# Transposes as 32x32 blocks through DRAM, half-width slice tokens and a table of steps for the order, in an f32 attention layer on one core

## The chip, the cores and the metric

One core of one Trainium2 chip. The time is the device time of one execution in microseconds (us), as a median over the runs of a kernel. Every kernel here gives the reference's result within the tolerance. Ratios are the mean time of one kernel's fast runs over that of the other's fast runs of the same rounds, so they are not quite the ratio of the medians quoted beside them.

## The reference, cut to what matters

For each of 32 batches x is 512 tokens by 256 features, f32. Two stages, each on a layernorm:

```
out = relu(x @ mlp1_w + b)                       # 512 x 512
out = elu(gat(out, no mask)) + out               # attention 512 x 512 over 512 features
out = relu(out @ mlp2_w + b)                     # 512 x 256
out = relu(elu(gat(out, adj)) + out)             # masked attention over 256 features
x   = x + out

w      = softmax((x @ W_x) @ W_slice / temp)     # per head, 8 heads x 64 slices
tokens = (w^T @ (x @ W_fx)) / (sum of w + 1e-5)  # 64 x 64 per head
attention among the 64 tokens of a head, then  out = w @ result @ W_out,  x = x + out
```

Every product in this kernel sums over the index that lies on partitions in both operands, so features and tokens have to change places several times in a batch. Those transposes are what the change is about.

## The kernel before: the parts that matter

The program is first recorded as a list of operations. A planner then orders the list: it simulates the five engines with a price for each operation, and on each engine takes the operation with the lowest "turn" among those that could start. The order it finds is fixed in the program; in the traces below each engine works down its own list and waits where something isn't there yet. (In all code cuts, `...` marks what is left out, and most comments are added for the reader.)

```python
class Recorder:
    AHEAD = 3                     # a batch may start while the oldest is at most 3 behind
    ORDERS = (1.0, 1.1, 1.2, 1.3, 1.4), (1.2, 1.4, 1.6), (0.0, 0.1, 0.2)

    def _cost(self, op, out, ins):               # (time on its engine, then time to be done)
        if op.method == "dma_start":
            return 0.1, 2.5 + out.size() * 4 / 180e3
        ...
    def order(self):              # 45 tries of two numbers a batch; the shortest by a replay wins
        ...
```

Most transposes are made on TensorE, written to PSUM and copied out by ScalarE. Two tensors, the first layernorm and the first attention's output, went another way already: VectorE turns 32x32 blocks, four writes put them into DRAM and one read brings them back in place.

```python
    def flip(src, stage, t):                      # 32x32 blocks on VectorE
        nc.vector.transpose(stage[:, :, ts(t, Q)], src.rearrange("p (c i) -> p c i", i=Q))

    def gather(stage, dst):                       # 4 writes to DRAM, 1 read back
        scr = dram.tile([blocks, Q, P // Q, P], F32, ...)
        for a in range(P // Q):
            nc.sync.dma_start(scr[:, :, a, :].rearrange("c r j -> r c j"), stage[ts(a, Q), :, :])
        nc.sync.dma_start(dst, scr.rearrange("(k c) r a j -> (c r) k (a j)", c=P // Q))
    ...
        # masked attention: e is turned by TensorE
            nc.scalar.activation(e, e, AF.Exp, bias=nmax[:, i : i + 1], accum_out=den[:, i : i + 1])
            pt = tr_tile([P, NT, P])
            for j in range(NT):
                nc.tensor.transpose(pt[:, j, :], e[:, ts(j)], ident)
            nc.scalar.copy(pT[:, :, ts(i)], pt)
    ...
        # slice tokens: full width, of which only the diagonal 64x64 blocks are used
        for p in range(NP):
            for k in range(KD):
                nc.tensor.matmul(pm[:, p, :], wfx[:, k, ts(p)], s1T[:, k, ts(p)], ...)
        nc.tensor.matmul(pm, bfx, nrow, start=False, stop=True)
```

## Time and profile before

| | before |
|---|---|
| time, median | 2928.01 us |
| TensorE busy | 98% |
| period of a batch | 88.5 us |
| matmuls a batch | 407 |
| DMA share of the span | 0.19 |
| first output leaves | 228.7 us |
| last masked-attention matmul to the end | 59.5 us |

In the views PE is TensorE, PEld its weight loads, DVE VectorE, ACT ScalarE, POOL GpSimd, and SP SyncE, which issues most transfers. The period is the distance of the output transfers in mid-span; all of it is TensorE work. The prediction shows the lines that say so.

### The profile page before, as it was taken

The numbers are of one execution on the slowest core, as the hardware profiler recorded it, in microseconds if no ns is written. First come the engines' busy times: TensorE is split into PE (matmuls) and PEld (weight loads), VectorE is DVE, ScalarE is ACT, GpSimd is POOL, SyncE is SP. The second block draws the span as 40 slices with busy tenths as digits, with TensorE's granted clock in tenths as the row PEclk, the third lists the DMA queues.
The fourth block names the chain that finished last, engine by engine and source line by source line (L and its number), as shares of the span: only waits on it lengthen the run. The fifth ranks groups of instructions, "written<-read, shape, count | busy, mean of one in ns | idle before, by whom it ended". The sixth has DMA issues, their size and how long they took to land.

```text
span 2926.5 us, 35159 instructions
## 1 busy us (share of the span) xinstructions
PE 2853.9 (98%) x13037; PEld 2187.4 (75%) x13037; DVE 1978.3 (68%) x4694; ACT 1119.3 (38%) x2182; POOL 112.8 (4%) x233
## 2 busy tenths in 40 slices
PE   3999999999999999999999999999999999999997
PEld 3777777777778777778777778777777777777775
DVE  4567776667776666776676866677766677766675
ACT  1433444333443343443333443333433334433432
POOL 1000000000000000000000000000000000000000
PEclk9999999999999999999999999999999999999998
DMA  5112220112211122211122211122201122201110
GB/s 177 44 29 65 65 65 22 52 57 65 65 53 34 44 65 65 65 44 44 44 65 65 65 36 51 44 65 65 65 26 54 51 65 65 61 19 45 43 44 15
DMA packets 185412, 159.34 MB, mean 54 GB/s; under 512 B 9109, under 2 KB 159257, under 8 KB 185241
## 3 DMA queue, kind: packets, MB, share of 16 engines
q1 hardware_dynamic: 181904, 154.96, 18.0%
q10 hardware_dynamic: 3336, 2.14, 0.3%
q8 instruction: 103, 1.69, 0.2%
q14 instruction: 69, 0.56, 0.1%
HBM read 89.96 MB, written 67.11 MB: 54 GB/s over the span
## 4 chain that ended last, share of the span: by engine, by line
PE 95%; DVE 3%; DMA 1%; ACT 0%; issue 0%; SPq 0%; POOL 0%; ACTq 0%; POOLq 0%; DVEq 0%
PE mm L255 85%; PE tr L255 9%; PE sm L255 1%; DVE w L255 1%; DVE mx L255 0%; DVE rs L255 0%; DMA wfx<-in_L_ffn_W_fx_dram 0%; DMA temp<-n_L_ffn_temperature_dram 0%; DVE m L255 0%; DVE u L255 0%; DMA scr<-xn_stage 0%; ACT m L255 0%; DMA xt<-in_x_dram 0%; DVE pT L255 0%; DVE ln_st L255 0%
## 5 line engine op out<-in xcount | busy, mean ns | idle before, releaser
L255 PE MATMUL mm<-wfc,o0T 128*128 128x257 f32 x2048 | 579.0, 381 | 0.0
L255 PE MATMUL mm<-h,pT 128*128 128x257 f32 (+1 forms) x2048 | 454.6, 378 | 0.1
L255 PEld LDWEIGHTS mm<-h,pT 128*128 128x128 f32 x2048 | 386.1, 189 | 80.5 <-issue 13.4
L255 PEld LDWEIGHTS mm<-wfc,o0T 128*128 128x128 f32 x2048 | 363.7, 190 | 53.2 <-issue 16.3
L255 PE MATMUL mm<-gg,wT 128*128 128x256 f32 x1024 | 299.5, 379 | 0.0
L255 PE MATMUL mm<-h,p2T 128*128 128x256 f32 x1024 | 290.8, 379 | 0.0
L255 PE MATMUL mm<-xnT,w 128*128 128x512 f32 x512 | 249.3, 592 | 0.0
L255 PE MATMUL mm<-xn,w 128*128 128x257 f32 x1024 | 246.4, 382 | 0.0
L255 PE MATMUL mm<-o1T,w 128*128 128x512 f32 x512 | 241.2, 592 | 0.0
L255 PE MATMUL mm<-weff,xn2T 128*128 128x512 f32 x512 | 226.7, 596 | 0.7 <-ACT xn2T L255 0.7
L255 DVE COPY h<-mm 128x257 f32<-128x257 f32 (+1 forms) x192 | 81.7, 425 | 208.2 <-PE mm L255 204.2
L255 PEld LDWEIGHTS mm<-gg,wT 128*128 128x128 f32 x1024 | 189.2, 190 | 24.0 <-ACT gg L255 0.2
L255 PEld LDWEIGHTS mm<-h,p2T 128*128 128x128 f32 x1024 | 186.6, 190 | 24.5
L255 PEld LDWEIGHTS mm<-xn,w 128*128 128x128 f32 x1024 | 186.0, 192 | 23.7 <-issue 3.3
L255 PEld LDWEIGHTS mm<-weff,xn2T 128*128 128x128 f32 x512 | 97.8, 191 | 122.9 <-issue 99.8
L255 ACT ACTIVATE m<-m 128x512 f32<-128x512 f32 x192 | 120.9, 630 | 170.7 <-DVE m L255 170.6
L255 DVE SCALAR_TENSOR_TENSOR u<-m,u 128x512 f32<-128x512 f32 x192 | 131.5, 685 | 70.3 <-ACT m L255 70.3
L255 ACT ACTIVATE u<-mm,rd 128x256 f32<-128x256 f32 x192 | 90.3, 470 | 208.0 <-PE mm L255 181.2
L255 ACT COPY h<-mm 128x257 f32<-128x257 f32 (+1 forms) x192 | 71.8, 374 | 227.2 <-PE mm L255 224.7
L255 PE MATMUL mm<-wh,o2T 128*128 128x258 f32 x512 | 155.6, 390 | 0.0
L255 ACT ACTIVATE w<-w 128x512 f32<-128x512 f32 x128 | 80.8, 631 | 187.6 <-DVE w L255 187.6
L255 ACT ACTIVATE o2T<-mm,b 128x512 f32<-128x512 f32 x64 | 44.0, 687 | 263.2 <-PE mm L255 262.9
(141 smaller groups left out, 4396.6 us busy)
## 6 DMA issues: line engine op xcount, KB each, us to landing
scr<-u_stage SPq DMA_DIRECT2D x128, 256.0 KB, 4.0
o1T<-scr SPq DMA_DIRECT2D x32, 1024.0 KB, 5.7
xt<-in_x_dram SPq DMA_DIRECT2D x32, 512.0 KB, 4.6
x<-in_x_dram SPq DMA_DIRECT2D x32, 512.0 KB, 4.1
scr<-xn_stage SPq DMA_DIRECT2D x128, 128.0 KB, 2.4
xnT<-scr SPq DMA_DIRECT2D x32, 512.0 KB, 6.4
out_dram<-x SPq DMA_DIRECT2D x32, 512.0 KB, 3.2
w<-in_L_gnn_mlp_w_dram SPq DMA_DIRECT2D x2, 512.0 KB, 6.8
```

Of the source, the lines that this page charges most:

```text
L255: getattr(getattr(self.nc, op.engine), op.method)(*op.args, **op.kwargs)
```

## The change

The intent is to take work from TensorE, the bound. The transposes of e, xn2, w and s1 leave TensorE for VectorE blocks and DRAM, in the manner of `flip` and `gather`. The masked product is turned round, so that its result comes out with features on partitions. The slice tokens are computed in halves of 64 columns, without the blocks that nobody uses. Copies and scalings move from VectorE to ScalarE, to make room. Left out of the cut below: w takes the buffer of p2T, the staging tiles of u, e and w share one buffer, and the rows of xn2 go through DRAM too, to match the block order. And the search over 45 orders gives way to a table with a turn for each of 23 steps. The core of the diff, with cuts:

```diff
+TURNS = {
+    "load": -152.1, "norm1": 325.7, "mlp1": 467.1, "h": 505.9, "factors": 512.7, "p": 531.2,
+    "pv": 533.5, "o1": 575.4, "mlp2": 575.4, "h2": 619.7, "e": 627.1, "p2": 627.1,
+    "pv2": 700.4, "x1": 718.3, "norm2": 735.4, "w": 763.7, "sums": 777.8, "s1T": 784.5,
+    "tokens": 830.6, "att": 855.6, "vo": 865.1, "gg": 867.3, "out": 893.5,
+}
+PERIOD, SPARE = 118.7, 0.01
...
         if op.method == "dma_start":
-            return 0.1, 2.5 + out.size() * 4 / 180e3
+            return 0.45, 2.2 + out.size() * 4 / 200e3
...
-            pt = tr_tile([P, NT, P])
-            for j in range(NT):
-                nc.tensor.transpose(pt[:, j, :], e[:, ts(j)], ident)
-            nc.scalar.copy(pT[:, :, ts(i)], pt)
+            nc.vector.tensor_scalar(e, e, rd, None, op0=OP.mult)
+            flip(e, stage, i)
+        nc.step = "p2"
+        gather("e", stage, pT)
...
+        for k in range(KD):
+            pm = mm_tile([P, N])
+            for j in range(NT):
+                nc.tensor.matmul(
+                    pm.rearrange("p (t a i) -> p t a i", t=NT, i=Q), h[:, j, ts(k)],
+                    in_order(pT[:, j, :]), start=(j == 0), stop=(j == NT - 1),
+                )
...
-            pt = tr_tile([P, NP, P])
-            for p in range(NP):
-                nc.tensor.transpose(pt[:, p, :], w[:, t, ts(p)], ident)
-            nc.scalar.copy(wT[:, :, ts(t)], pt)
+            flip(wt, stage, t)
+        gather("w", stage, wT)
...
-        for k in range(KD):
-            pt = tr_tile([P, INNER])
-            for p in range(NP):
-                nc.tensor.transpose(pt[:, ts(p)], s1[:, p, ts(k)], ident)
-            nc.scalar.copy(s1T[:, k, :], pt)
+        gather("s1", stage, s1T)
...
+                for s in range(2):
+                    nc.tensor.matmul(
+                        pm[ts(s, C), p, :].rearrange("c (a i) -> c a i", i=Q),
+                        wfx[:, k, ts(2 * p + s, C)], in_order(s1T[:, k, :])[:, p, ts(s, 2), :],
+                        start=(p == 0 and k == 0), stop=False,
+                    )
```

More of the change, by code (lines that the diff above doesn't have):

```diff
@@ L1 @@
 from contextlib import ExitStack
-from itertools import product
 import concourse.bass as bass
@@ L28 @@
     AHEAD = 3
-    ORDERS = (1.0, 1.1, 1.2, 1.3, 1.4), (1.2, 1.4, 1.6), (0.0, 0.1, 0.2)
     def __init__(self, nc):
-        self.nc, self.ops, self.logs, self.age, self.stage = nc, [], {}, -1, 0
+        self.nc, self.ops, self.logs, self.age, self.step = nc, [], {}, -1, ""
         for engine in ENGINES:
@@ L63, in take @@
                 (outs if key in ("out", "accum_out") else ins).append(x)
-        op = _Op(engine, method, args, kwargs, self.age, self.stage, len(self.ops))
+        op = _Op(engine, method, args, kwargs, self.age, self.step, len(self.ops))
         op.cost, op.lag = self._cost(op, outs[0], ins)
@@ L72, in take @@
                 log = self.logs.setdefault(ap.tensor.name, _Log(ap, self.age))
-                op.logs.add(log)
+                if log not in op.logs:
+                    op.logs.append(log)
                 kept = []
@@ L97, in _cost @@
         if op.method == "dma_start":
-            return 0.1, 2.5 + out.size() * 4 / 180e3
+            return 0.45, 2.2 + out.size() * 4 / 200e3
         if op.engine == "tensor":
             one = max(n / 1200 + 0.002, 0.109)
+            if out.ap[0][1] == P // 2:
+                one = max(n / 2400, 0.03)
             return (one if op.method == "transpose" else 2 * one), self.DRAIN
@@ L195, in _schedule @@
         return done
-    def _length(self, ops):
-        free, ready, users, until, slots, held = {}, {}, {}, {}, {}, set()
-        for op in ops:
-            for log in op.logs:
-                users[log] = users.get(log, 0) + 1
-        for op in ops:
-            at = ready.get(op, 0.0)
-            for log in op.logs:
-                if log not in held:
-                    held.add(log)
-                    places = slots.setdefault(log.tag, [0.0] * log.bufs)
-                    places.sort()
-                    at = max(at, places.pop(0))
-            t = free.get(op.engine, 0.0)
-            t = max(t + (0.03 if op.engine == "tensor" and at > t - 0.1 else 0.0), at)
-            free[op.engine], end = t + op.cost, t + op.cost + op.lag
-            for log in op.logs:
-                users[log] -= 1
-                until[log] = max(until.get(log, 0.0), end)
-                if not users[log]:
-                    slots[log.tag].append(until[log] + self.SIGNAL)
-            for later in op.after:
-                if later.engine != op.engine:
-                    at = end + self.SIGNAL
-                else:
-                    at = t + op.cost if op.engine == "tensor" else end
-                ready[later] = max(ready.get(later, 0.0), at)
-        return max(free.values())
     def order(self):
@@ L232, in order @@
         for op in self.ops:
-            stage = op.age, op.stage
-            parts[op] = work.get(stage, 0.0)
-            work[stage] = parts[op] + (op.cost if op.engine == "tensor" else 0.0)
-        best = None
-        for late, long, spare in product(*self.ORDERS):
-            turns = {
-                op: op.age + (late + long * part / work[op.age, 1] if op.stage else
-                              part / (work[op.age, 0] or 1.0))
-                for op, part in parts.items()
-            }
-            try:
-                ops = self._schedule(self.ops, turns.get, spare)
-            except RuntimeError:
-                continue
-            length = self._length(ops)
-            if best is None or length < best[0]:
-                best = length, ops
-        self.length = best[0]
-        return best[1]
+            step = op.age, op.step
+            parts[op] = work.get(step, 0.0)
+            work[step] = parts[op] + (op.cost if op.engine == "tensor" else 0.02)
+        ends = dict(zip(TURNS, list(TURNS.values())[1:] + [max(TURNS.values())]))
+        turns = {}
+        for op, part in parts.items():
+            at = TURNS.get(op.step, 0.0)
+            part /= work[op.age, op.step]
+            turns[op] = op.age * PERIOD + at + part * (ends.get(op.step, 0.0) - at)
+        return self._schedule(self.ops, turns.get, SPARE)
     def emit(self):
@@ L264, in __init__ @@
         self.psum = ap.space == bass.MemoryType.PSUM
-        self.queue = self.tag, age if self.psum else 0
+        self.queue = self.tag, age if self.psum or self.tag.startswith("stage") else 0
         self.entries = []
 class _Op:
-    def __init__(self, engine, method, args, kwargs, age, stage, index):
+    def __init__(self, engine, method, args, kwargs, age, step, index):
         self.engine, self.method, self.args, self.kwargs = engine, method, args, kwargs
-        self.age, self.stage, self.index = age, stage, index
-        self.logs, self.after = set(), []
+        self.age, self.step, self.index = age, step, index
+        self.logs, self.after = [], []
     def __lt__(self, other):
@@ L359, in flip, with gather @@
         )
-    def gather(stage, dst):
+    def gather(what, stage, dst):
         blocks = stage.shape[1]
-        scr = dram.tile([blocks, Q, P // Q, P], F32, name="scr", tag=f"scr{blocks}", bufs=2)
+        scr = dram.tile([blocks, Q, P // Q, P], F32, name="scr", tag=f"scr_{what}", bufs=2)
         for a in range(P // Q):
@@ L474, in adj_ffn_kernel @@
                 )
-    adjt = new("adjt", [P, NT, N], tag="w", dtype=I32)
+    adjt = new("adjt", [P, NT, N], tag="wT", dtype=I32)
     nc.sync.dma_start(adjt, adj.rearrange("(t p) j -> p t j", p=P))
@@ L583, in elu_elu @@
     def elu_elu(parts, m, u):
-        (v0, rd0, cols0), (v1, rd1, cols1) = parts
-        nc.vector.tensor_scalar(u[:, cols0], v0, rd0, None, op0=OP.mult)
-        nc.scalar.activation(u[:, cols1], v1, AF.Copy, scale=rd1)
+        for v, rd, cols in parts:
+            nc.scalar.activation(u[:, cols], v, AF.Copy, scale=rd)
         nc.vector.tensor_scalar(m, u, 0.0, None, op0=OP.min)
@@ L595, in front @@
     def front(b):
-        load_x(b + 1)
+        nc.step = "load"
+        if b:
+            load_x(b)
+        nc.step = "norm1"
         xn = new("xn", [P, NT, D])
@@ L603, in front @@
         xnT = new("xnT", [P, KD, N])
-        gather(stage, xnT)
+        gather("xn", stage, xnT)
+        nc.step = "mlp1"
         o0T = new("o0T", [P, KH, N], bufs=2)
@@ L613, in front @@
             nc.scalar.activation(o0T[:, m, :], pm, AF.Relu, bias=b1[:, m : m + 1])
+        nc.step = "h"
         h = new("h", [P, NT, 2, HH + 1])
@@ L623, in front @@
                     )
-                if s:
-                    nc.vector.tensor_copy(h[:, t, s, :], pm)
-                else:
-                    nc.scalar.copy(h[:, t, s, :], pm)
+                nc.scalar.copy(h[:, t, s, :], pm)
         f1, f2 = h[:, :, 0, HH], h[:, :, 1, HH]
+        nc.step = "factors"
         fm = small("fm", [P, 1])
@@ L657, in front @@
             nc.scalar.copy(acb[:, s, :], pt)
+        nc.step = "p"
         pT = new("pT", [P, NT, N])
         for j in range(NT):
-            nc.vector.tensor_scalar(
-                pT[:, j, :], acb[:, 1, :], ex[:, 3, j : j + 1], None, op0=OP.mult
+            nc.scalar.activation(
+                pT[:, j, :], acb[:, 1, :], AF.Copy, scale=ex[:, 3, j : j + 1]
             )
@@ L667, in front @@
             )
+        nc.step = "pv"
         o1T = new("o1T", [P, KH, N])
-        stage = new("u_stage", [P, HID // Q, P], tag="p2T")
+        stage = new("u_stage", [P, HID // Q, P], tag="stage")
         for i in range(NT):
@@ L683, in front @@
             flip(u, stage, i)
-        gather(stage, o1T)
+        nc.step = "o1"
+        gather("u", stage, o1T)
         for m in range(KH):
@@ L690, in middle @@
     def middle(b, o1T):
+        nc.step = "mlp2"
         o2T = new("o2T", [P, KD, N])
@@ L700, in middle @@
             nc.scalar.activation(o2T[:, m, :], pm, AF.Relu, bias=b2[:, m : m + 1])
+        nc.step = "h2"
         h = new("h2", [P, NT, D + 2])
@@ L707, in middle @@
                 )
-            if t % 2:
-                nc.vector.tensor_copy(h[:, t, :], pm)
-            else:
-                nc.scalar.copy(h[:, t, :], pm)
+            nc.scalar.copy(h[:, t, :], pm)
         f2b = new("f2b", [P, N])
@@ L716, in middle @@
         nc.scalar.copy(f2b, pt)
-        r2 = new("r2", [P, NT, D])
-        for t2 in range(NT // 2):
-            pt = tr_tile([P, 2, D])
-            for s in range(2):
-                for k in range(KD):
-                    nc.tensor.transpose(pt[:, s, ts(k)], o2T[:, k, ts(2 * t2 + s)], ident)
-            nc.scalar.copy(r2[:, ts(t2, 2), :], pt)
         pT = new("p2T", [P, NT, N])
+        nc.step = "e"
+        stage = new("e_stage", [P, N // Q, P], tag="stage")
         den = small("den", [P, NT])
@@ L739, in middle @@
             )
-            pt = tr_tile([P, NT, P])
-            for j in range(NT):
-                nc.tensor.transpose(pt[:, j, :], e[:, ts(j)], ident)
-            nc.scalar.copy(pT[:, :, ts(i)], pt)
-        rd = small("rd2", [P, NT])
-        nc.vector.reciprocal(rd, den)
+            rd = den[:, i : i + 1]
+            nc.vector.reciprocal(rd, rd)
+            nc.vector.tensor_scalar(e, e, rd, None, op0=OP.mult)
+            flip(e, stage, i)
+        nc.step = "p2"
+        gather("e", stage, pT)
@@ L747, in middle @@
         x1 = new("x1", [P, NT, D], bufs=2)
         nc.sync.dma_start(x1, x[b].rearrange("(t p) d -> p t d", p=P))
-        for i2 in range(NT // 2):
-            pm = mm_tile([P, 2, D])
-            for s in range(2):
-                i = 2 * i2 + s
-                for j in range(NT):
-                    nc.tensor.matmul(
-                        pm[:, s, :], pT[:, j, ts(i)], h[:, j, :D],
-                        start=(j == 0), stop=(j == NT - 1),
-                    )
-            u, m = row("u2", (P, 2, D)), row("m2", (P, 2, D))
-            elu_elu(
-                [(pm[:, s, :], rd[:, 2 * i2 + s : 2 * i2 + s + 1], s) for s in range(2)], m, u
-            )
-            nc.vector.tensor_tensor(u, u, r2[:, ts(i2, 2), :], op=OP.add)
+        nc.step = "pv2"
@@ new lines, in middle @@
+        for k in range(KD):
[5 more added lines that the diff above has]
+                )
+            m = row("m2")
+            nc.vector.tensor_scalar(m, pm, 0.0, None, op0=OP.min)
+            nc.scalar.activation(m, m, AF.Exp)
+            nc.scalar.activation(m, m, AF.Exp, bias=neg1)
+            nc.vector.scalar_tensor_tensor(m, m, -1.0, pm, op0=OP.add, op1=OP.max)
+            nc.vector.tensor_tensor(o2T[:, k, :], m, o2T[:, k, :], op=OP.add)
@@ L763, in middle @@
+        nc.step = "x1"
+        for t2 in range(NT // 2):
+            pt = tr_tile([P, 2, D])
+            for s in range(2):
+                for k in range(KD):
+                    nc.tensor.transpose(pt[:, s, ts(k)], o2T[:, k, ts(2 * t2 + s)], ident)
             nc.vector.scalar_tensor_tensor(
-                x1[:, ts(i2, 2), :], u, 0.0, x1[:, ts(i2, 2), :], op0=OP.max, op1=OP.add
+                x1[:, ts(t2, 2), :], pt, 0.0, x1[:, ts(t2, 2), :], op0=OP.max, op1=OP.add
             )
@@ L768, in back @@
     def back(b, x1):
-        xn = new("xn2", [P, NT, D + 1])
+        nc.step = "norm2"
+        xn = new("xn2", [P, NT, D])
+        layernorm(x1, xn, "ln2")
+        stage = new("xn2_stage", [P, D // Q, P], tag="stage4")
+        for t in range(NT):
+            flip(xn[:, t, :], stage, t)
+        xnT = new("xn2T", [P, KD, N])
+        gather("xn2", stage, xnT)
+        scr = dram.tile([NT, P, D], F32, name="scr", tag="rows", bufs=4)
+        nc.sync.dma_start(scr.rearrange("t p d -> p t d"), xn)
+        xn = new("xn2_rows", [P, NT, D + 1])
         nc.gpsimd.memset(xn[:, :, D : D + 1], 1.0)
-        layernorm(x1, xn, "ln2")
-        xnT = new("xn2T", [P, KD, N])
-        transpose_features(xn, xnT)
-        w = new("w", [P, NT, INNER])
+        for t in range(NT):
+            nc.sync.dma_start(xn[ts(t, Q), :, :D], scr[t].rearrange("(a i) d -> i a d", i=Q))
+        nc.step = "w"
+        w = new("w", [P, NT, INNER], tag="p2T")
         wT = new("wT", [P, NP, N])
+        stage = new("w_stage", [P, INNER // Q, P], tag="stage")
         for t in range(NT):
@@ L798, in back @@
             )
-            pt = tr_tile([P, NP, P])
-            for p in range(NP):
-                nc.tensor.transpose(pt[:, p, :], w[:, t, ts(p)], ident)
-            nc.scalar.copy(wT[:, :, ts(t)], pt)
+            flip(wt, stage, t)
+        gather("w", stage, wT)
+        nc.step = "sums"
         s1 = new("s1", [P, NP, D + 1])
+        stage = new("s1_stage", [P, D // Q, P], tag="stage4")
         for p in range(NP):
@@ L814, in back @@
             nc.vector.reciprocal(rn, rn)
-            nc.vector.tensor_scalar(s1[:, p, :], pm, rn, None, op0=OP.mult)
+            nc.scalar.activation(s1[:, p, :], pm, AF.Copy, scale=rn)
+            flip(s1[:, p, :D], stage, p)
+        nc.step = "s1T"
         s1T = med("s1T", (P, KD, INNER))
-        for k in range(KD):
-            pt = tr_tile([P, INNER])
-            for p in range(NP):
-                nc.tensor.transpose(pt[:, ts(p)], s1[:, p, ts(k)], ident)
-            nc.scalar.copy(s1T[:, k, :], pt)
+        gather("s1", stage, s1T)
         pn = sm_tile([NP, P])
         nc.tensor.transpose(pn, s1[:, :, D], ident)
-        nrow = new("nrow", [NP, NP, P])
-        nc.vector.tensor_tensor(
-            nrow, ident[:NP, :NP, None].to_broadcast([NP, NP, P]),
-            pn[:, None, :].to_broadcast([NP, NP, P]), op=OP.mult,
-        )
-        pm = mm_tile([P, NP, P])
+        nrow = new("nrow", [NP, 2, NP, G])
+        for s in range(2):
+            nc.vector.tensor_tensor(
+                nrow[:, s], ident[:NP, :NP, None].to_broadcast([NP, NP, G]),
+                pn[:, None, ts(s, G)].to_broadcast([NP, NP, G]), op=OP.mult,
+            )
+        nc.step = "tokens"
+        pm = mm_tile([P, NP, G])
         for p in range(NP):
             for k in range(KD):
-                nc.tensor.matmul(
-                    pm[:, p, :], wfx[:, k, ts(p)], s1T[:, k, ts(p)],
-                    start=(p == 0 and k == 0), stop=False,
-                )
-        nc.tensor.matmul(pm, bfx, nrow, start=False, stop=True)
+                for s in range(2):
+                    nc.tensor.matmul(
+                        pm[ts(s, C), p, :].rearrange("c (a i) -> c a i", i=Q),
+                        wfx[:, k, ts(2 * p + s, C)], in_order(s1T[:, k, :])[:, p, ts(s, 2), :],
+                        start=(p == 0 and k == 0), stop=False,
+                    )
+        for s in range(2):
+            nc.tensor.matmul(
+                pm[ts(s, C)], bfx[:, ts(s, C)], nrow[:, s], start=False, stop=True
+            )
         def diagonal(dst, src):
@@ L845, in back @@
         tok = new("tok", [P, NP, G])
-        diagonal(lambda s: tok[ts(s, C), :, :], lambda s: pm[ts(s, C), :, ts(s, G)])
+        nc.vector.tensor_copy(tok, pm)
         for s in range(2):
@@ L854, in back @@
             nc.tensor.matmul(psc[:, p, :], qbd[:, p, :], tok[:, p, :], start=True, stop=True)
+        nc.step = "att"
         amax = small("amax", [P, NP])
@@ L867, in back @@
         nc.vector.reciprocal(ra, ra)
+        nc.step = "vo"
         vo = med("vo")
@@ L881, in back @@
         nc.vector.tensor_copy(attT, pt)
+        nc.step = "gg"
         gg = med("gg")
@@ L892, in back @@
                 )
+        nc.step = "out"
         for t2 in range(NT // 2):
@@ L907, in adj_ffn_kernel @@
     for b in range(B):
-        nc.age, nc.stage = b, 0
-        o1T = front(b)
-        nc.stage = 1
-        back(b, middle(b, o1T))
+        nc.age = b
+        back(b, middle(b, front(b)))
     with tc.manual_schedule():
```

## The prediction

> **What bounds the kernel now.** I read the page's busy shares first, then the busy time of two stretches that are one batch long, then the order of the matmuls inside one batch, the groups that the change removes, the groups that it adds more of, and the transfers.
>
> ```profile
> span 2926.5 us, 35159 instructions
> PE 2853.9 (98%) x13037; PEld 2187.4 (75%) x13037; DVE 1978.3 (68%) x4694; ACT 1119.3 (38%) x2182; POOL 112.8 (4%) x233
> ```
>
> ```profile
> 1500.00:1588.50 88.50, 88.50 (x408) 67.95 (x407) 61.38 (x146) 34.90 (x68) 3.42 (x7) 1.00 0.19 54
> 2500.00:2588.50 88.50, 88.50 (x407) 67.94 (x406) 61.28 (x146) 34.90 (x68) 3.41 (x7) 1.00 0.19 54
> ...
> 2870.00:2890.00 20.00, 13.28 (x39) 7.29 (x40) 13.24 (x29) 3.01 (x6) 1.26 (x2) 0.74 0.00 0
> 2890.00:2910.00 20.00, 17.09 (x79) 12.79 (x78) 10.01 (x27) 4.71 (x9) 0.79 (x2) 0.86 0.00 1
> 2910.00:2927.00 17.00, 10.45 (x46) 7.99 (x44) 3.46 (x7) 2.48 (x6) 0.00 (x0) 0.90 0.09 31
> ```
>
> The columns are the stretch, its length, then busy time and count of PE, PEld, DVE, ACT and POOL, the granted clock, and the DMA share and rate. The 13037 matmuls over 32 batches are 407 each, and every 88.5 us stretch holds 407: the period of a batch is 88.5 us, PE is busy all of it, DVE 61.3, ACT 34.9. Thirty-two periods are 2832 us; the other 94 us are 43 us before the first matmul, which waits for weights, and the last batch's thinner end, where PE idles and its clock drops to 0.74. So TensorE's own issue sets the period.
>
> A matmul's duration isn't what it costs the stream; the step between starts is:
>
> ```profile
> 1572.22 7.03 PE L255 MATMUL mm<-weff,xn2T 128*128 128x512 f32 x16
> 1579.09 1.88 PE L255 MATMUL mm<-xnT,w 128*128 128x512 f32 x4
> 1580.81 0.60 PE L255 MATMUL mm<-wfc,o0T 128*128 128x257 f32 x2
> 1581.24 0.60 PE L255 MATMUL tr<-ident,w 128*128 128x128 f32 x4
> 1581.67 1.90 PE L255 MATMUL mm<-xn,w 128*128 128x257 f32 x8
> ```
>
> From start to start: 16 of 512 columns take 6.87 us, 0.429 each; 2 of 257 take 0.43, 0.216 each; 4 transposes take 0.43, 0.108 each. With these steps the 407 matmuls of a batch add up to 87.8 us of the 88.5.
>
> **What the Trainium skill says.** (1) "Perfetto Trace Analysis", section "Identifying the Most-Contended Engine": matmul busy share overstates how near the roofline a kernel is, since matmuls are pipelined; load-weights busy share is the better sign. Here that is 75%, yet the starts are back to back, so I count steps between starts instead. (2) "VectorE: DVE Perf Modes", section "The three transpose paths": VectorE transposes only inside 32x32 blocks. That is why the blocks must be put in place by a transfer through DRAM; the kernel before does so for two tensors already. (3) The same page, "Why PSUM operands drop a tier": a PSUM source loses the double rate of a scalar operation. The trace agrees: the minimum over 512 columns from SBUF takes 415 ns, while a scaling of only 256 columns from PSUM takes 474. (4) "TensorEngine Tiling (Array Packing)", section "Key Properties": changing the tiling mode drains TensorE. A related sign in the trace is the bias product with only four rows: its two matmuls of 512 columns hold the stream 1.05 us (1515.08 to 1516.13) instead of 0.86, with 0.1 us of gap before.
>
> **The change part by part.**
>
> TensorE, removed:
>
> ```profile
> L255 PE MATMUL tr<-ident,w 128*128 128x128 f32 x512 | 78.5, 277 | 9.6 <-DVE rs L255 6.6 <-DVE w L255 2.9
> L255 PE MATMUL tr<-ident,e 128*128 128x128 f32 x512 | 76.8, 273 | 0.0
> ...
> L255 PE MATMUL tr<-ident,s 128*128 128x128 f32 x256 | 43.6, 273 | 0.4 <-DVE s L255 0.3
> L255 PE MATMUL tr<-ident,xn 128*128 128x128 f32 x256 | 39.7, 278 | 9.4 <-DVE xn L255 9.4
> ```
>
> These are 16+16+8+8 = 48 transposes a batch, at 0.108 us 5.2 us. The transposes of o2T stay, moved behind the second attention. The turned masked product is 16 matmuls of 512 columns (6.86 us) in place of 32 of 256 (6.9): nothing. The slice tokens by halves replace 16 matmuls of 128 columns (1.8 us) and the bias pair (1.15 with its gap) by 32 half-width matmuls of 64 columns and 4 half-width bias ones. No trace shows the half-width step. As an estimate between 64/1200 us (half the step of 128 columns) and half of that, if neighbouring halves overlap, the 32 take 0.9 to 1.7 us and the bias 0.4 to 0.9, to which drains are added at each switch of mode: before, this block was interleaved with other work in about six pieces, and at 0.1 to 0.3 us a piece that is 0.6 to 1.8. Net between -1.4 and +1.5; I take -0.5. TensorE goes from 88.5 to about 82.8 us a batch.
>
> VectorE, added:
>
> ```profile
> L255 DVE STREAM_TRANSPOSE u_stage<-u 128x512 f32<-128x512 f32 x128 | 88.9, 695 | 0.3
> ...
> L255 DVE STREAM_TRANSPOSE xn_stage<-xn 128x256 f32<-128x256 f32 x128 | 49.0, 421 | 3.3 <-DMA scr<-xn_stage 3.3
> ```
>
> Four flips each of e and w (8 x 0.695 = 5.56) and of xn2 and s1 (8 x 0.421 = 3.37); the scaling of e (4 x 0.478, from the row that makes pT, = 1.9); three more reciprocals (0.45); the minimum from PSUM (2 x 0.27 = 0.5); nrow in two (0.2). Sum 12.0. Taken away: six scalings of u (6 x 0.474 = 2.8), the copies of h and h2 (4 x 0.425 + 2 x 0.426 = 2.55), the first product of pT (1.9) and the scaling of s1 (1.9). Sum 9.2. VectorE goes from 61.3 to about 64 us, 77% of the new period. ScalarE loses the copies of the transposes of e, w, xn2, s1 and r2 out of PSUM (14 x 0.585 = 8.2), two scalings (0.94) and one copy of tok (0.37), 9.5 in all. It gains 8.9 from what VectorE gave up. It stays near 34 us.
>
> Transfers:
>
> ```profile
> scr<-u_stage SPq DMA_DIRECT2D x128, 256.0 KB, 4.0
> o1T<-scr SPq DMA_DIRECT2D x32, 1024.0 KB, 5.7
> ...
> scr<-xn_stage SPq DMA_DIRECT2D x128, 128.0 KB, 2.4
> xnT<-scr SPq DMA_DIRECT2D x32, 512.0 KB, 6.4
> ```
>
> Out and back, e and w add 2 MB each, xn2 and s1 1 MB each, the rows of xn2 1 MB: 7 MB a batch, 235 MB on 159 MB. The DMA share rises from 0.19 to about 0.47: not a bound. Issues rise from 13 to 38 a batch, at 0.377 us 14 us of SP's time.
>
> What lies on the path is latency. A removed transpose with its copy took about 2.3 us at the end of the trace (s1, from 2897.5 to 2899.9); flip, landing in DRAM and landing in SBUF are 0.4 + 2.4 + 6.4 = 9.2 us for 512 KB and 0.7 + 4.0 + 5.7 = 10.4 for 1 MB. In the steady state four batches are in flight and this is hidden if the order leaves TensorE other work. In the last batch there is none: xn2 and s1 each add about 7 us, the moved transposes 1 to 2; w's transfer lies beside the sums and tokens. The end grows by 16 us. Filling the deeper pipeline I put at 8 us, and leftover bubbles in the steady state, with VectorE busier and an order fixed from modelled times, at 0.4 us a batch, 13 us.
>
> Sum: 2928 - 32 x 5.2 (166) - 32 x 0.5 (16) + 16 + 8 + 13 = 2783; I say 2780 us, 5% less.
>
> **The rivals.** First, a buffer cycle becomes the bound. p2T and w now share one single buffer, and w needs the result of p2T through the norm, so gather of e, second attention, norm, transfer of xn2, slice weights and sums run one after another once a batch. In the steady state before, from the first matmul on p2T (1536.66) to the last of the sums (1591.2) are 54.5 us; add 5.7 for the gather of e and about 8 for xn2's transfer: 69 us of 82.8. It fits with 14 us to spare; for it speaks also that the weights stage keeps its pace though VectorE is shared. Against it: u, e and w flips take turns in one stage buffer, some 18 us each by the trace, and a wait there stretches the cycle. If it becomes 88, the time is 2880 to 2950.
>
> Second, SP issues in order, so one transfer that waits for its data holds all behind it. The page now has the gathers waiting on their own scratch writes; with six gathers a batch, late transfers could cost a few us each: 2 us a batch makes 2850. For it speaks that the order is taken from modelled landings; against it, that modelled landings of 1 MB are longer than the measured 5.7.
>
> Third, the drains of half-width matmuls give back what the transposes saved: at the dear end +1.5 us a batch, 2845.
>
> Fourth, everything fits and the halves overlap: -1.4 in place of -0.5 and no bubbles, 2735.
>
> **Range and chances.** The range 2715 to 2860 holds the fourth rival and the mild forms of the second and third, not a closed buffer cycle. Within 2% begins at 2870. Faster 0.88, same 0.09, slower 0.03.
>
> **What would show it.** Right: about 361 matmuls a batch (407 - 48 - 16 + 18), a period near 83 us with PE busy in nearly all of it, DVE near 64 us, DMA share near 0.47, the chain of waits still almost all PE. Wrong: PE share well under 97% in mid-span with its waits ending at transfers or at w and p2T (first or second rival); gaps or long steps around the products of s1T and wfx (third); a first out transfer much later, or an end longer than some 80 us after the last p2T matmul, would show that fill or tail was misjudged.

## More of the kernel before

Columns: stretch, length, busy time (and count) of PE, PEld, DVE, ACT and POOL, granted clock, DMA share, GB/s.

```profile
1563.00:1587.00 24.00, 24.00 (x94) 15.77 (x93) 22.59 (x55) 11.36 (x19) 2.52 (x4) 1.00 0.43 122
```

## The result, and the profile after

3021.48 us (3016.19 to 3025.93, 4 runs) against 2928.01: a ratio of 1.0319, 95% interval 1.0297 to 1.0340. Slower, where 5% faster was predicted. Page of the changed kernel:

```profile
span 3014.1 us, 33327 instructions
## 1 busy us (share of the span) xinstructions
PE 2784.2 (92%) x11565; PEld 1922.1 (64%) x11565; DVE 2017.3 (67%) x4822; ACT 1095.0 (36%) x2214; POOL 112.8 (4%) x233
```

TensorE has 1472 matmuls fewer, 361 a batch, and still the span is longer: it is busy 92% and no longer 98%. VectorE is busy 39 us longer than before, ScalarE 24 us less. The output transfers are 90.4 us apart in mid-span, where 82.8 was predicted. So what grew isn't work: TensorE stands 230 us of its span in place of 73. The view of waits, longest TensorE ones first (in us: total, times, longest):

```profile
PE mm L225 <- DMA s1T<-scr: 92.5, 32, 12.6
PE tr L225 <- DMA wx<-in_L_ffn_W_x_dram: 37.0, 1, 37.0
PE mm L225 <- DMA p2T<-scr: 25.4, 20, 6.4
PE mm L225 <- DVE pT L225: 24.3, 30, 5.0
```

The second is the start and was there before. The first comes in every batch: TensorE stands 2.9 us for s1T, the turned sums on their way back from DRAM. TensorE's timeline around one such wait (start, length, instruction, idle before it and its releaser):

```profile
1575.65 5.39 PE L225 MATMUL mm<-p2T,h 128*128 128x512 f32 x12 [0.54 <-DMA p2T<-scr]
1583.45 0.45 PE L225 MATMUL mm<-s1T,wfx 128*64 128x64 f32 x8 [2.41 <-DMA s1T<-scr]
1583.83 1.12 PE L225 MATMUL mm<-p2T,h 128*128 128x512 f32 x2
1584.89 0.45 PE L225 MATMUL mm<-s1T,wfx 128*64 128x64 f32 x8
```

TensorE had more to do: two of the p2T matmuls come right after. They stand behind the first s1T products because the planner put them there, and the list is fixed. The two then take 1.06 us from start to start where 0.86 is usual.

Why s1T is late shows in SyncE's timeline of the same stretch (start, time of the issues, transfers):

```profile
1563.46 3.12 SPq L225 DMA_DIRECT2D scr<-w_stage  x4
1566.69 1.12 SPq L225 DMA_DIRECT2D p2T<-scr  x1
1567.94 1.70 SPq L225 DMA_DIRECT2D scr<-s_stage  x2
1570.58 0.79 SPq L225 DMA_DIRECT2D wT<-scr  x1
1571.41 1.28 SPq L225 DMA_DIRECT2D scr<-s_stage  x2
1572.74 3.62 SPq L225 DMA_DIRECT2D scr<-xn_stage  x4
1579.71 0.38 SPq L225 DMA_DIRECT2D s1T<-scr  x1
```

Within ten microseconds come 1 MB of w, two gathers of 1 MB, and the four writes of s1 between them. The s1 writes, 128 KB each, land 7 to 8 us after their issue, and only then can s1T be read back. The list of transfers (KB each, median us to landing) has the same for the whole run:

```profile
p2T<-scr SPq DMA_DIRECT2D x32, 1024.0 KB, 9.0
...
wT<-scr SPq DMA_DIRECT2D x32, 1024.0 KB, 8.9
...
scr<-s_stage SPq DMA_DIRECT2D x128, 128.0 KB, 7.8
```

The prediction had 5.7 us for 1 MB and 2.4 us for 128 KB, from a kernel in which transfers met few others. The stretches of the changed kernel, the burst and the rest of the batch:

```profile
1563.00:1587.00 24.00, 20.74 (x90) 13.90 (x89) 16.21 (x48) 9.47 (x18) 1.37 (x3) 1.00 0.88 257
1587.00:1653.00 66.00, 65.66 (x278) 45.96 (x277) 47.44 (x106) 24.61 (x51) 2.06 (x4) 1.00 0.33 94
```

A mean DMA share of 0.47 is 0.88 for a quarter of the batch and 0.33 for the rest. In the quarter, TensorE is idle 3.3 us; in the rest, 0.3.

**Theory A.** The work did fall as predicted. The order is what fails: the planner prices each transfer as if it were alone (0.45 + 2.2 + 0.66 = 3.3 us for a 128 KB write), puts what reads it that close behind, and the burst makes each landing late by the same amount in every batch.

**Rivals.** B: a cycle through the shared single buffers, or VectorE, holds the period whatever the order is. C: the half-width products drain TensorE at each change of width and give back what the transposes saved. D: the step table is a worse order than the old search.

### The profile page after: what moved, and what is told of

The parts are those of the page before. It is cut to its first block, busy times and chain, and to the rows that moved or that the text cites. A ratio compares the mean times of both kernels' runs of the same rounds, so it can differ in the third digit from the quotient of the medians.

```text
span 3014.1 us, 33327 instructions
## 1 busy us (share of the span) xinstructions
PE 2784.2 (92%) x11565; PEld 1922.1 (64%) x11565; DVE 2017.3 (67%) x4822; ACT 1095.0 (36%) x2214; POOL 112.8 (4%) x233
## 5 line engine op out<-in xcount | busy, mean ns | idle before, releaser
L225 PE MATMUL mm<-h,pT 128*128 128x256 f32 (+1 forms) x2048 | 510.4, 385 | 30.3 <-DVE pT L225 24.3
L225 PE MATMUL mm<-wfc,o0T 128*128 128x257 f32 x2048 | 498.2, 380 | 0.0
L225 PE MATMUL mm<-p2T,h 128*128 128x512 f32 x512 | 265.5, 654 | 35.7 <-DMA p2T<-scr 25.4
L225 DVE SCALAR_TENSOR_TENSOR e<-f2b,h,mbias 128x512 f32<-128x512 f32 x128 | 92.9, 747 | 280.2 <-ACT f2b L225 280.2
L225 PE MATMUL mm<-xn_rows,w 128*128 128x257 f32 x1024 | 259.2, 388 | 13.4 <-DVE w L225 5.5
L225 ACT COPY h<-mm 128x257 f32<-128x257 f32 (+1 forms) x384 | 143.7, 375 | 244.5 <-PE mm L225 236.8
L225 PEld LDWEIGHTS mm<-xn_rows,w 128*128 128x128 f32 x1024 | 198.2, 194 | 47.1 <-ACT w L225 9.1
L225 PEld LDWEIGHTS mm<-p2T,h 128*128 128x128 f32 x512 | 94.6, 200 | 130.6 <-issue 81.0
L225 PEld LDWEIGHTS mm<-o1T,w 128*128 128x128 f32 x512 | 95.8, 191 | 115.5 <-issue 85.0
L225 PE MATMUL mm<-s1T,wfx 128*64 128x64 f32 x1024 | 68.7, 252 | 92.5 <-DMA s1T<-scr 92.5
```

The source lines that it names most:

```text
L225: getattr(getattr(self.nc, op.engine), op.method)(*op.args, **op.kwargs)
```

## The experiments

They were run with the kernel before beside them (medians 2927.76 to 2928.83 us). The changed kernel itself was not run again; times are compared with its 3021.48. Each expectation names its own theories A and B, which are not always the A and B above; where the letters differ, the text says so.

### 1. Slice tokens in full width again

```diff
-                for s in range(2):
-                    nc.tensor.matmul(
-                        pm[ts(s, C), p, :].rearrange("c (a i) -> c a i", i=Q),
-                        wfx[:, k, ts(2 * p + s, C)], in_order(s1T[:, k, :])[:, p, ts(s, 2), :], ...
+                nc.tensor.matmul(
+                    pm[:, p, :].rearrange("c (a i) -> c a i", i=Q),
+                    wfx[:, k, ts(p)], in_order(s1T[:, k, :])[:, p, :, :], ...
```

> The changed kernel with one part undone: the slice tokens again as 8 full-width products (16 matmuls of 128 columns) and one bias product, of which only the diagonal blocks are kept. Theory A (drains at the switches between half-width and full-width matmuls cost about 2.5 us a batch, more than the halves save): about 40 to 70 us faster than the changed kernel, 2950 to 2980 us, while the wait for s1T stays at about 3 us a batch. Theory B (only waits for transfers matter; halves cost what their issue costs): 1 to 1.5 us a batch more TensorE work in the stream, so the same time or 20 to 40 us slower, 3020 to 3060 us.

(Theory A of this expectation is C above, its B is A above.) 3001.55 us (ratio to before 1.0260, 1.0242 to 1.0277), 20 us faster; the period fell from 90.4 to 89.5, the wait for s1T stayed (97.4 us). C has the right sign and a fifth of the size that it would need: in this order the halves cost 0.9 us a batch net. I had expected 40 to 70 us from the drains; the time falls between the two ranges. They can't be the main cause of the loss.

### 2. The writes of s1 from another issuing engine

```diff
-            nc.sync.dma_start(
+            (nc.scalar if what == "s1" else nc.sync).dma_start(
                 scr[:, :, a, :].rearrange("c r j -> r c j"), stage[ts(a, Q), :, :]
```

> The changed kernel, with only the four scratch writes of s1 issued from ScalarE instead of SyncE; same bytes, same order of all else. Theory A (transfers of one issuing engine are served in order[...], so the s1 writes wait behind the 1 MB gathers of p2T and of wT issued just before): the writes land in 3 to 4 us instead of 7.8, the wait of TensorE for s1T falls from 92 us in all to under 30, time 2930 to 2960 us. Theory B (the 16 DMA engines are simply busy in this burst, whatever the queue, or SyncE's own issue is the limit): the writes still take 6 to 8 us, the wait stays over 70 us, time 3000 to 3030.

2983.92 us (1.0191, 1.0176 to 1.0206), between the two ranges. The landing did not get shorter:

```profile
scr<-s_stage ACTq DMA_DIRECT2D x128, 128.0 KB, 8.5
```

So the detailed form of A (theory A of this expectation), a queue served in order, falls: a write from a second queue waits just as long behind the same burst. The Trainium skill says as much in "DMA: Bandwidth & Descriptors", section "Issuing engines are not separate DMA queues": transfers run on the same 16 engines and interleave whoever issues them, and another issuer saves issue time only. The trace agrees: the last of the four was issued 4.5 us after the last block of s1 was turned, behind other issues of SyncE (0.45 to 1.2 us each) and its wait for the w writes; now it is 2.5 us. Of this only half a microsecond reaches s1T, which lands 15.5 us after that block in place of 16.0 (medians over 16 batches of mid-span). The wait for s1T fell from 92.5 to 74.7 us, and the time by 37 us. The rest of the gain isn't shown; the clock is a part of it (in the 1900 us from 600 to 2500 it was granted at half for 17 us, in the changed kernel for 48).

### 3. The gather of wT after that of s1T

The 1 MB gather of wT is needed only by the output product, much later. It is recorded after s1's gather, and the planner is told that it follows it.

```diff
-        gather("w", stage, wT)
+        collect_w = gather("w", stage, wT, late=True)      # the four writes alone
 ...
         gather("s1", stage, s1T)
+        first = nc.ops[-1]
+        collect_w()                                        # the 1 MB read
+        first.after.append(nc.ops[-1])
```

> The changed kernel, with the 1 MB gather of wT, which nothing needs before the output product, issued after the gather of s1T instead of before two of the s1 writes. Theory A (transfers queue behind each other): the wait for s1T falls from 92 us in all to under 20; time 2920 to 2950 us. Theory B (the delay is in latency of each transfer or in the issue rate): wait stays over 60 us, time 2990 to 3020.

2950.09 us (1.0073, 1.0058 to 1.0088), 71 us faster by moving one transfer. The wait for s1T:

```profile
PE mm L225 <- DMA s1T<-scr: 12.6, 17, 9.4
```

from 92.5 to 12.6 us, as A had it, with TensorE's list nearly the same (72 of its 11565 places differ); 2950.09 is the upper edge of what it had expected. The s1 writes still take 7.2 us, behind p2T's gather. What TensorE gained at s1T it lost in part at xnT, whose gather now meets the burst (27.4 us of waits, 2.1 before): the list still holds places that were planned for transfers without company.

### 4. The half-width products as one block

```diff
+            if op.half:                                    # TensorE, output of 64 partitions
+                turns[op] -= 1e4
```

> The changed kernel with the half-width matmuls of a batch issued as one block without full-width matmuls between them; no work is changed. Theory A (each switch of width drains TensorE): the steps around them lose about 1.5 to 2 us a batch, though the wait for s1T may grow by up to 0.8 us as less other work is left in front; time 2980 to 3005 us. Theory B (half-width matmuls are dear by themselves, not at the switches): 3010 to 3040 us.

3031.01 us (1.0356, 1.0335 to 1.0376), slower, outside what theory A of this expectation (the drains, C above) had, and inside the range of its theory B, that halves are dear by themselves; run 7 will refute that. The wait for s1T grew to 118.1 us in all, 0.8 us a batch, as was to be feared, since the block needs everything at once. But more was lost behind the wait. The stretches of the wait, of the 5 us after it, and of the next 5:

```profile
1572.50:1576.00 3.50, 0.19 (x3) 0.11 (x4) 1.98 (x3) 1.35 (x2) 0.00 (x0) 1.00 0.71 201
1576.00:1581.00 5.00, 5.00 (x40) 2.64 (x41) 1.02 (x2) 0.00 (x0) 1.18 (x2) 0.66 0.93 276
1581.00:1586.00 5.00, 5.00 (x14) 2.27 (x13) 0.69 (x1) 1.27 (x3) 0.00 (x0) 1.00 0.52 181
```

After 3.3 us of idleness the mean granted clock is 0.66 in the next 5 us. The Trainium skill has this in "TensorE: Matmul & The Clock Gate", Part 1: TensorE's clock is halved after an idle window of about 3.4 us, and comes back after a busy one. The trace agrees: its clock is granted at 0.5 in stretches of 3.41 us or a multiple of it. So a wait of this length costs more than itself. As a test of C the run is spoilt by that; C is decided by runs 1 and 8.

### 5 to 8. The same instructions in an order planned with other prices

Nothing in these kernels differs from the changed kernel but the planner's numbers, and in run 8 the tokens of run 1. First, transfers that share one path (the three numbers are from the changed kernel's trace):

```diff
-            return 0.45, 2.2 + out.size() * 4 / 200e3
+            return 0.6, out.size() * 4 / 270e3
 ...
             op.start, op.end = t, t + op.cost + op.lag
+            if op.method == "dma_start":
+                pipe = max(pipe, t + op.cost) + op.lag
+                op.end = pipe + 1.7
```

> The changed kernel with only the planner's price of a transfer altered: an issue costs 0.6 us, and transfers follow each other through one shared path at 270 GB/s, landing 1.7 us after their turn (numbers read from the changed kernel's trace), in place of a latency of its own for each. All instructions stay the same, only their order on the engines differs. Theory A (the order is planned as if transfers did not delay each other, so TensorE stands at fixed places for late landings): TensorE's waits for s1T and p2T fall from 118 us to under 50, time 2890 to 2950 us. Theory B (a cycle through shared buffers or VectorE sets the period whatever the order): waits move elsewhere, time 2990 to 3050 us.

2886.61 us (0.9859, 0.9844 to 0.9874): 135 us faster than the changed kernel, and 1.4% below the kernel before. The waits for s1T and p2T fell from 118 to 63 us, less than expected; the time fell more, to just under the range.

Then only the window, five batches in flight in place of four:

```diff
-    AHEAD = 3
+    AHEAD = 4
```

> The changed kernel with only the planner's window widened, so that five batches rather than four may be in flight; prices of the transfers unaltered. Theory A (order blind to shared transfers): some of the wait goes, as more other work can stand between the sums and the tokens: 2940 to 2990 us. If the window itself is what holds the kernel back: under 2900. If neither: 3010 to 3030.

2925.10 us (0.9994, 0.9975 to 1.0013), 96 us faster, more than A had expected; the wait for s1T is still 50.5 us. Presumably another batch in flight gives the planner other work to put in front of the late products, though it doesn't know that they are late.

Both together:

> Both: shared price of transfers and the wider window. Theory A: waits of TensorE for transfers under 30 us in all, period near 84 us, time 2820 to 2890 us, faster than the kernel before. Theory B: over 2950 us.

2795.86 us (0.9547, 0.9532 to 0.9561), 226 us faster than the changed kernel and 4.5% faster than the kernel before. That is below the expected range, though TensorE's waits for transfers are 44 us without the start and not under 30. This is the run that decides: same instructions, same buffers, same bytes, in another order on every engine. Its page, and TensorE's two longest waits:

```profile
span 2795.1 us, 33319 instructions
## 1 busy us (share of the span) xinstructions
PE 2669.1 (95%) x11565; PEld 1904.2 (68%) x11565; DVE 2019.8 (72%) x4822; ACT 1091.9 (39%) x2214; POOL 128.4 (5%) x233
```

```profile
PE mm L228 <- DMA xnT<-scr: 37.1, 1, 37.1
PE mm L228 <- DMA p2T<-scr: 27.9, 24, 9.4
PE mm L228 <- DMA s1T<-scr: 11.1, 1, 11.1
```

The first is the start. The period is 83.0 us. The transfers are hardly quicker than in the changed kernel: the s1 writes land after 7.4 us, p2T after 9.0, and the burst is still there (the densest 24 us of this batch, from 1528 us, have a DMA share of 0.90). They are expected to be that slow, so TensorE does other work meanwhile, and s1T holds it up only once, in the first batch. In the same place in the order:

```profile
1555.54 1.02 PE L228 MATMUL mm<-xnT,w 128*128 128x512 f32 x2
1556.49 1.15 PE L228 MATMUL mm<-s1T,wfx 128*64 128x64 f32 x32
1557.57 0.65 PE L228 MATMUL mm<-nrow,bfx 4*64 4x256 f32 x4
1558.15 1.12 PE L228 MATMUL mm<-xnT,w 128*128 128x512 f32 x2
```

s1T was issued at 1550.64, the products start at 1556.49 with no wait, and as all have their data by then, they run as one block: 1.66 us for 36 half-width matmuls.

And this order with the tokens in full width:

> The same with the slice tokens again in full width. Theory A with costly width switches, as the run with full tokens showed (20 us faster): 2800 to 2870 us and 10 to 20 us faster than with halves. If the switches cost nothing when nothing waits at them: 10 to 40 us slower than with halves.

2829.56 us (0.9662, 0.9646 to 0.9678): 34 us slower than with halves, period 84.1 against 83.0. So where nothing waits at them, the halves save 1.1 us a batch, and in the changed kernel's order the same halves cost 0.9. That settles C: the price of the width switches depends on into how many pieces the order cuts the block, about 7 a batch in the changed kernel and 1 in run 7, counted in the traces from 600 to 2500 us.

Runs 1 and 8 also say how much of the gain hangs on this. With the tokens in full width, the new order gains 172 us (3001.55 to 2829.56). With halves it gains 226; so about 54 us of the 226 hang on the halves, which save time in one block and cost it in seven pieces, and not on the waits alone.

How the 7.4 us a batch between the changed kernel and run 7 are made up: the time from each matmul's start to the next one's start, summed by group over 21 batches of mid-span. A wait counts for the group in front of it.

| group | changed, us a batch | run 7 | difference |
|---|---|---|---|
| masked product (p2T), with the wait for s1T behind it | 10.76 | 6.94 | 3.82 |
| output product (gg), with the wait for pT | 7.73 | 6.95 | 0.78 |
| first attention (pT), with the wait for p2T | 15.26 | 14.77 | 0.49 |
| half-width products and bias | 2.96 | 1.66 | 1.30 |
| transposes of o2T, put between them | 1.34 | 0.88 | 0.46 |
| first product (xnT) | 7.60 | 7.18 | 0.42 |
| all others | 44.75 | 44.64 | 0.11 |

The same 1900 us of mid-span, first of the changed kernel, then of run 7 (columns as above):

```profile
600.00:2500.00 1900.00, 1809.84 (x7558) 1247.83 (x7557) 1312.43 (x3129) 715.84 (x1449) 72.07 (x147) 0.99 0.47 134
600.00:2500.00 1900.00, 1882.32 (x8246) 1350.19 (x8245) 1429.45 (x3409) 777.84 (x1577) 93.13 (x161) 1.00 0.52 147
```

TensorE's idle time is 90 us, or 4.3 a batch, in the changed kernel (2.6 for s1T, 0.7 for pT, 0.5 for p2T) and 0.8 a batch in run 7. So about half of the 7.4 us is idle time. The clock was granted at half for 48 of the 1900 us in the changed kernel, which is worth at most 1.1 us a batch, and never in run 7.

### 9 and 10. The old search in place of the table

```diff
-        ends = dict(zip(TURNS, ...))                # a turn for each step, from the table
+        for late, long, spare in product(*self.ORDERS):   # the search of the kernel before
```

> The changed kernel's data flow, ordered by the search of the kernel before (two stages a batch, 45 tries, one chosen) instead of the step table; prices of transfers unaltered. If the step table is at fault for the loss: faster than the changed kernel, under 2980 us. If the fault lies in the prices of the transfers and the table itself is better than the old search: slower than the changed kernel, 3030 to 3120 us.

3127.60 us (1.0681, 1.0659 to 1.0703): 106 us slower than the changed kernel. D falls: for this data flow and these prices the table is much the better order. (A little beyond the expected range; part of the loss is the clock, granted at half for 154 of the 1900 us.)

> The same search, but with the shared price of transfers and the window of five batches, as in the run of 2796 us. If the table carries part of that gain: 2960 to 3060 us, at least 150 us slower than 2796. If the price and the window alone carry it: 2780 to 2850 us.

3107.43 us (1.0606, 1.0590 to 1.0622), slower than I had expected of either theory. With the old search, the new price and the wider window bring only 20 us; with the table, 226. But this run does not test the old search with good prices: each of the 45 orders is planned with the shared path, while the replay that picks the shortest of them was left as it was. In it a transfer lands its bytes over 270 GB/s after its issue, 0.5 us for 128 KB, without the path and without the 1.7 us. Nor is there the same lateness to plan for: in runs 9 and 10 the s1 writes land after 4.6 and 5.7 us and p2T after about 5.5, and TensorE still waits 70 and 83 us for s1T. Whether a right price needs the table is not shown.

### 11. The table moved

> The version of 2796 us (shared price, window of five batches) with its table of steps moved by a random search against the modelled end. Theory: what is left are a wait for p2T (28 us in all) and the thin ends, so little is to be had: 2750 to 2790 us. If the model is no guide any more at this level: 2790 to 2830.

2778.66 us (0.9484, 0.9468 to 0.9500), the fastest version, 5.2% faster than the kernel before. The table was moved by a random search against the planner's own model with the shared path. In this run the wait for p2T is 12.4 us in all, down from 27.9.

### 12. A longer price, but no sharing

```diff
-            return 0.45, 2.2 + out.size() * 4 / 200e3
+            return 0.6, 3.3 + out.size() * 4 / 190e3
```

> The changed kernel with the window of five batches, and with each transfer priced by a longer latency of its own (0.6 us to issue, then 3.3 us plus its bytes at 190 GB/s: 4.6 us for 128 KB to 9.4 us for 1 MB, about the measured landings on average) but not by a shared path. If it is the sharing that the plan must know: clearly slower than the 2796 us of the shared price, 2840 to 2920 us, with a wait for s1T left, since the s1 writes take over 7 us and not 4.6. If any longer price does: 2785 to 2830 us.

2833.11 us (0.9675, 0.9659 to 0.9691), between the two ranges and nearer to that of "any longer price does". Against 2925.10 of the same window with the short price, 92 of the possible 129 us come from the longer price alone. I had expected a wait for s1T to stay; it did not (14.5 us in all, nearly all of it in the first batch), and from 600 to 2500 us the view of waits lists none of TensorE's at all. The period is 83.8 us and not 83.0, and the trace shows where: this order cuts the half-width block into 5 pieces a batch, of which these are the first three:

```profile
1570.61 0.56 PE L225 MATMUL mm<-s1T,wfx 128*64 128x64 f32 x10
1571.10 1.12 PE L225 MATMUL mm<-xnT,w 128*128 128x512 f32 x2
1572.16 0.45 PE L225 MATMUL mm<-s1T,wfx 128*64 128x64 f32 x6
1572.53 1.12 PE L225 MATMUL mm<-p2T,h 128*128 128x512 f32 x2
1573.59 0.45 PE L225 MATMUL mm<-s1T,wfx 128*64 128x64 f32 x8
```

Its products of s1T take 1.78 us from start to start in place of 1.08, and the groups put between the pieces 0.2 us more each, while the first attention takes 0.8 less. So the other 37 us are not shown to come from the sharing; to keep TensorE from waiting, the plan had to know only that landings take long.

## Why the prediction was wrong, step by step

- **Work of TensorE, 82.8 us a batch**: right. The count is 361; with an order that hardly waits the period is 83.0.
- **VectorE near 64, ScalarE near 34, DMA share 0.47**: right: 62.4, 34.1 and 0.47 (busy time from 600 to 2500 us, scaled to 90.4).
- **Halves, -0.5 between -1.4 and +1.5**: both signs came true, +0.9 in the changed kernel's order and -1.1 in run 7's.
- **Fill and end, 24 us**: right in sum for the changed kernel, too small for run 7. What isn't period is 3014 - 32 x 90.4 = 121 us, 27 more than before; in run 7 it is 139, 45 more. Both signs of misjudgement that the prediction named came: the first output leaves at 286.7 us in place of 228.7, and from the last masked-attention matmul to the end are 83.4 us in place of 59.5, over the 80 that it set.
- **"leftover bubbles in the steady state, with VectorE busier and an order fixed from modelled times, at 0.4 us a batch, 13 us"**: this is the term that failed. TensorE's idle time in mid-span is 4.3 us a batch in place of 0.4, 3.2 of it for transfers. The period is 7.6 us above the work predicted: 4.3 are this idle time, 1.4 are the halves (+0.9 in place of -0.5), at most 1.1 the slow clock after long waits, and a little under 1 us is not accounted for.
- Behind it stands **"The DMA share rises from 0.19 to about 0.47: not a bound"**. As a mean that holds. But the transfers of four batches meet in 24 us, with a share of 0.88, and landing times are 1.6 times (1 MB) to 3.2 times (128 KB) those of the kernel before.
- **The second rival** named the mechanism, transfers late against an order taken from modelled landings, at 2 us a batch. I let it go because "modelled landings of 1 MB are longer than the measured 5.7". The 5.7 us were measured where few other transfers ran; the change itself made them 9.0. The rival had it that a transfer waiting in SyncE's list holds those behind it. That has a part (runs 2 and 3 changed little but the issue of transfers and gained 37 and 71 us), but the time is lost where TensorE's fixed list stands, and another order takes it back with landings as long as before.
- **The first rival**, the closed cycle of p2T and w, did not come about: the same buffers run at 83.0 us. (Its sum of 54.5, 5.7 and 8 is 68, not 69.)

## What to carry to other kernels

When work is moved from a busy engine to transfers, don't judge by the mean DMA share: look at the share in the densest stretch of a period, and price each transfer with what is in flight beside it. In a program whose order is fixed beforehand, a landing that is later than planned can cost time in every period, even if the waiting engine has other work right behind; here it was 2.6 us of 90. So re-plan with the landing times of the changed kernel's own trace before judging the change itself: here the new price alone turned 3% slower into 1.4% faster, and with one more batch in flight into 4.5% faster, with not one instruction altered. And look at what else a new order changes: about 54 of those 226 us hang on a block of half-width products that was no longer cut into pieces.

## What the Trainium skill lacked or had wrong

- "DMA: Bandwidth & Descriptors" gives a transfer's time as a fixed part plus its bytes, measured for transfers issued from GpSimd. It has no landing time for a small transfer in company: a 128 KB write landed after 2.4 us in the kernel before and after 7.8 us in a burst with a DMA share of 0.88.
- The same page calls the sequencer's time to issue a transfer usually small, without a number for a burst. A single SyncE issue took 0.38 us, and those in a row 0.45 to 1.2 us; moving four issues a batch to another engine saved 37 us (1.2%), while the landings stayed as long (8.5 us).
- "TensorEngine Tiling (Array Packing)" says that a change of tiling mode drains TensorE, but not what it costs. In the changed kernel the products of s1T, the bias and the o2T transposes took 4.3 us a batch cut into pieces, and 2.5 us as one block in run 7, for the same matmuls. The slow clock explains little of this: in run 3, cut into about as many pieces and with the full clock from 600 to 2500 us, they took 4.2.
- "VectorE: DVE Perf Modes", section "The three transpose paths", has no row for blocks put together through DRAM. Here, 48 TensorE transposes of 0.108 us a batch were replaced by it; with the half-width tokens, which saved 1.1 us of it, the period fell from 88.5 to 83.0 us once the order allowed for 7 to 9 us of landing.
